# Gated cross-attention and quantized FFN on one core: softmax two steps ahead of its transposes, projections one to a step, the stage behind the attention and the first layer's order written in the source

## Chip, cores and metric

The kernel runs on one core of one Trainium2 chip. The metric is the device time of one execution in microseconds (us), start to end. The kernel before took 717.9 us, the median of three runs (715.8, 717.9, 718.52).

## What is computed

The inputs are x of 2 x 2048 rows with 512 columns, a context of 2 x 77 rows with 512 columns, two gates, and the weights. In short:

```python
x = x + tanh(g_xattn) * attention(layernorm(x), ctx, ctx, Wq, bq, Wk, bk, Wv, bv, Wo, bo)
x = x + tanh(g_ffn) * ffn(layernorm(x), w1, b1, w2, b2)
```

The attention has 16 heads of 32 columns, 77 keys, scores divided by sqrt(32), an ordinary softmax over the keys, and an output projection. The FFN has 2048 hidden columns and quantizes what it multiplies:

```python
def quant(x):
    scale = maximum(max(abs(x)), 1e-6) / 127
    return round(x / scale), scale
def qlinear(x, w, b):
    xq, sx = quant(x)
    wq, sw = quant(w)
    return (xq @ wq.T + b[None, :]) * (sw * sx)
o = qlinear(gelu(qlinear(x, w1, b1)), w2, b2)
```

The scale belongs to the whole tensor. So the first layer can start only when the maximum of all 4096 normalized rows is known, and the second only when the maximum of the whole hidden tensor is known.

## The kernel before

**Tiling.** The 4096 rows are cut into 8 blocks of 512 rows; a block is four tiles of 128 rows. The kernel has three stages: the attention over all blocks, the first layer over all blocks, the second layer over all blocks. The hidden tensor does not fit on the chip beside the rest: the last 8 of its 32 pieces are held, the other 24 go to memory (h, L611) and come back as Gb (L630).

**A block of the attention** has eight steps s (loop at L428 and L429). Step s stands for group g = s // 2 of four heads and for one half (two tiles) of the rows. What a step works on:

- softmax (L258): the scores ps on PE (L267), their maximum mx on DVE (L276), the subtraction into e on DVE (L280), the exponential on ACT (L286), the sum sm on DVE (L288), its reciprocal (L290), and the product e times rs on POOL (L291).
- transpose_a (L297), twice a step: four transposes pta of e on PE (L304), copied to aT by ACT (L305).
- project_q (L245), once for a group: four matmuls pq (L248) and a copy with bias to qT on ACT (L256).
- apply_v (L307), once for a group: pc on PE (L313), copied to cT by ACT (L321).
- project_o (L323), once for a row tile of the block before: four matmuls po (L326); DVE adds the result to x (L333).

For the next block, norm(i+1) (L222) takes the statistics of its rows on DVE (st_a and L141), and transpose_x (L229) normalizes a row tile on DVE (xn, L234), transposes it on PE (ptx, L239) and copies it to xnT on ACT (L240). At step 7, norm2_stats and norm2_max (L337, L342) take the second layernorm's statistics (st_f) of the block before and the maxima of its normalized rows: a burst of DVE work. Through weight_step (L388) DVE also prepares the FFN's weights in the odd steps of four blocks: maxima of w1 in block 1 (L374), quantization of w1 in block 2, maxima of w2 in block 3, quantization of w2 in block 4. At step 0 of blocks 2 and 4, scale_of (L148) makes the scale of the weights: a maximum over columns on DVE, a diagonal on DVE, a matmul with ones on PE that brings the 128 maxima into every row, then maximum, scale and inverse on DVE. add_bias (L242) is POOL's.

**Which step has what.** In step s the softmax of step s + 1 is issued first, then the first transposes of step s. project_q of groups 1, 2, 3 stands at steps 0, 2, 4, and that of the next block's group 0 at step 6; apply_v of the block before's group 3 at step 0 and of groups 0, 1, 2 at steps 2, 4, 6; project_o at steps 1, 3, 5, 6; norm(i+1) at step 3; transpose_x, two tiles each, at steps 5 and 6.

**What sets the order.** Each engine runs its queue in order, and the order is fixed when the program is built. For the opening, the source's order is kept on DVE and PE (manual_schedule, L409). All else is ordered by a list scheduler of the framework, which works with estimated durations; `with tc.issue_after(x)` keeps the instructions in it behind x on their engine. Tiles come from rotating pools, and a new tile waits until the last use of the one whose place it takes. In the attention PSUM has two slots for transposes (ps_t), two for projections (ps_p) and two for scores (ps_s). The pools in SBUF hold 3 of e, 5 of qT, 3 of aT, 7 of cT, 1 of xnT. The 8 places of a 1 MB block (xpool) are shared by the blocks of x and the raw weights.

**Behind the attention** (L491 to L501) come apply_v of the last group, the four project_o of block 7 and, tile by tile, their statistics and maxima. Then the rows of block 0 are made ready for the first layer: normalize_x (L526) on POOL (xs, L529), scale_of for x, and quantize_x (L539), which for block 0 goes tile by tile: multiply and add a large constant, then subtract it again so that the value is rounded (DVE L167 and L168; ACT L546 and DVE L547 for tiles 2 and 3), four transposes px on PE (L553), copy to xqT on ACT (L556).

**The first layer** (L570): for each block, 16 chunks of the hidden columns, in four groups a of four chunks. A chunk is four matmuls ph (L583), the gelu on ACT (L590), and for two chunks together the maximum hmax on DVE (L600). For the block that follows, DVE normalizes (xs, L529), quantizes in two instructions of 2048 elements (L167, L168), and copies the transposed tiles (xqT, L558); PE does the 16 transposes px (L553) wherever the scheduler puts them. px has two slots (ps_x), ph two of two banks.

**The second layer** quantizes h (ACT L636, DVE hq L637), multiplies (pf, L645), adds b2 on POOL (L659) and the product to x (DVE), and stores. It begins with the two held blocks.

Of the kernel before, what the change touches and what calls it, by code (L numbers as in the profile page):

```python
# [8 lines left out]
F32 = mybir.dt.float32  # L9
# [33 lines left out]
def tile_flamingo_gated_block(  # L43
# [50 lines left out]
    bv_sb = awts.tile([NK, D], F32, name="bv_sb")  # L94
# [5 lines left out]
    b2_sb = const.tile([P, D], F32, name="b2_sb")  # L100
# [17 lines left out]
    nc.sync.dma_start(b2_sb, b2.to_broadcast([P, D]))  # L118
# [10 lines left out]
    w1q = const.tile([P, KC, FF], BF16, name="w1q")  # L129
    w2q = const.tile([P, FC, D], BF16, name="w2q")  # L130
# [33 lines left out]

    def quantize(dst, src, inv):

        nc.vector.tensor_scalar(src, src, inv, MAGIC, ALU.mult, ALU.add)  # L167
        return nc.vector.tensor_scalar(dst, src, MAGIC, None, ALU.subtract).ins  # L168
# [5 lines left out]
    with actx:  # L174
        work = actx.enter_context(tc.tile_pool(name="work", bufs=2))
# [4 lines left out]
        kblk, vblk = [], []  # L180
        for b in range(B):
            kb = awts.tile([P, NG, RK], F32, name=f"kb{b}")
            nc.gpsimd.memset(kb, 0.0)
            kblk.append(kb)
            vblk.append(awts.tile([NK, D], F32, name=f"vb{b}"))
# [56 lines left out]
        def add_bias(i, t):  # L242
            nc.gpsimd.tensor_tensor(X[i][:, t, :], X[i][:, t, :], bo_sb, ALU.add)
# [98 lines left out]
        def norm2_max(i, t0=0, t1=NT):  # L342

            tm = small.tile([P, NT], F32, tag="tm", name=f"tm{i}_{t0}")
            for t in range(t0, t1):
                xn = work.tile([P, D], F32, tag="xn", name=f"xf{i}_{t}")
                nc.vector.tensor_scalar(
                    xn,
                    X[i][:, t, :],
                    mean2[:, i, t, 0:1],  # L350
                    rstd2[:, i, t : t + 1],
                    ALU.subtract,
                    ALU.mult,
                )
                nc.vector.tensor_reduce(
                    tm[:, t - t0 : t - t0 + 1], xn, AX.X, ALU.max, apply_absolute_value=True
                )
            k = i if t1 - t0 == NT else NB - 1 + t0
            nc.vector.tensor_reduce(xmax[:, k : k + 1], tm[:, : t1 - t0], AX.X, ALU.max)
# [67 lines left out]
        softmax(0, 0)  # L427
        for i in range(NB):  # L428
            for s in range(2 * NG):  # L429
                last = None  # L430
                if s + 1 < 2 * NG:
                    last = softmax(i, s + 1)
                    last_product = last["POOL"]
                elif i + 1 < NB:
                    last = softmax(i + 1, 0)
# [4 lines left out]
                if s == 0:  # L440
                    if i > 0:
                        apply_v(i - 1, NG - 1)
                    project_q(i, 1)
# [9 lines left out]
                if s in (2, 4):  # L453
                    project_q(i, 1 + s // 2)
                    apply_v(i, s // 2 - 1)
                if s in (1, 3, 5, 6) and i > 0:
                    project_o(i - 1, (1, 3, 5, 6).index(s))
                if s == 6:
                    apply_v(i, 2)
                if i + 1 < NB:  # L460
                    if s == 3:
                        with tc.issue_after(last["DVE"]):
                            norm(i + 1)
                    if s in (5, 6):
                        for t in (2 * s - 10, 2 * s - 9):
                            transpose_x(i + 1, t)
                transpose_a(i, s, 1)
                if s == 6 and i + 1 < NB:
                    project_q(i + 1, 0)
# [8 lines left out]
                if last is not None:  # L478
                    with tc.issue_after(last["DVE"]):
                        weight_step(i, s)  # L480
                    t = s - NT if i == 0 else s // 2
                    if t >= 0 and (i == 0 or s % 2 == 0):
                        with tc.issue_after(last["POOL"]):
                            add_bias(i, t)
# [10 lines left out]
        for t in range(NT):  # L495
            project_o(NB - 1, t)
            last = norm2_stats(NB - 1, t, t + 1)
            if t > 0:
                with tc.issue_after(last):
                    norm2_max(NB - 1, t - 1, t)  # L500
        norm2_max(NB - 1, NT - 1, NT)  # L501
# [6 lines left out]
    )  # L508

# [7 lines left out]
    with ExitStack() as fctx:  # L517
# [8 lines left out]
        def normalize_x(i, engine):  # L526
            xs = fwork.tile([P, NT, D], F32, tag="xs", name=f"xs{i}")
            for t in range(NT):
                engine.tensor_scalar(  # L529
                    xs[:, t, :],  # L530
                    X[i][:, t, :],
                    mean2[:, i, t, 0:1],
                    rstd2[:, i, t : t + 1],
                    ALU.subtract,
                    ALU.mult,
                )
            return xs

        def quantize_x(i, xs, n):  # L539

            xq = fwork.tile([P, NT, D], BF16, tag="xq", name=f"xq{i}")
            xqT = fwork.tile([P, KC, TB], BF16, tag="xqT", name=f"xqT{i}")
            for t0 in range(0, NT, n):
                v, vq = xs[:, t0 : t0 + n, :], xq[:, t0 : t0 + n, :]
                if n == 1 and t0 >= NT // 2:
                    nc.scalar.activation(v, v, AF.Copy, bias=MAGIC, scale=inv_x)  # L546
                    last = nc.vector.tensor_scalar(vq, v, MAGIC, None, ALU.subtract).ins  # L547
                else:
                    last = quantize(vq, v, inv_x)
                for t in range(t0, t0 + n):  # L550
                    px = ps_x.tile([P, KC, P], BF16, tag="px", name=f"px{i}_{t}")
                    for kc in range(KC):
                        nc.tensor.transpose(px[:, kc, :], xq[:, t, kc * P : (kc + 1) * P], identb)  # L553
                    dst = xqT[:, :, t * P : (t + 1) * P]
                    if n == 1:
                        nc.scalar.copy(dst, px)  # L556
                    else:
                        nc.vector.tensor_copy(dst, px)  # L558
            return xqT, last


        with tc.issue_after(last_product), tc.high_priority(offset=300):
            xs = normalize_x(0, nc.gpsimd)
        s_x, inv_x = scale_of(xmax, "x", ps_g, "pg")
        xqT, last = quantize_x(0, xs, 1)
# [3 lines left out]
        nc.vector.tensor_scalar(b1s, b1_sb, s1, None, ALU.mult)  # L569
        for i in range(NB):  # L570
            cur = xqT
            if i + 1 < NB:
                with tc.issue_after(last):
                    xs = normalize_x(i + 1, nc.vector)
                xqT, last = quantize_x(i + 1, xs, NT)
            for a in range(GT):
                G = gtile(f"G{i}_{a}")
                for v in range(GF // 2):
# [149 lines left out]
```

## Time and profile before

The profile is of one execution, which itself took 718.17 us; 716.2 us of it is the span from the first to the last instruction recorded. The mean TensorE clock was 0.986 of full speed.

| engine | busy us | share of the span | instructions |
|---|---|---|---|
| PE (matmul) | 662.0 | 92% | 3160 |
| PEld (weight load) | 326.6 | 46% | 3160 |
| DVE | 526.9 | 74% | 821 |
| ACT | 345.7 | 48% | 474 |
| POOL | 210.7 | 29% | 164 |

| group of instructions | count | mean ns of one |
|---|---|---|
| PE ph, first layer (L583) | 512 | 381 |
| PE pf, second layer (L645) | 512 | 386 |
| PE pq (L248) | 256 | 613 |
| PE po (L326) | 256 | 597 |
| DVE mx (L276) | 64 | 786 |
| DVE sm (L288) | 64 | 789 |
| DVE hmax (L600) | 65 | 1196 |
| ACT exp (L286) | 64 | 716 |
| ACT gelu (L590) | 128 | 777 |
| POOL product e (L291) | 64 | 1218 |
| DVE xs, first layer (L529) | 24 | 540 |
| DVE quantize, multiply and add (L167) | 7 | 1281 |
| DVE quantize, subtract (L168) | 7 | 1218 |
| DVE xqT copy (L558) | 28 | 416 |

A duration in such a row is from an instruction's start to its end, and ends of matmuls are modelled; neighbours on an engine overlap a little, so where one follows another without a pause the distance from start to start is shorter than the mean. The attention takes 0 to 429 us, its last projections 429.11 to 443.11, the first layer 457.57 to 585.07, the second the rest. By DMA 85.44 MB are moved, 119 GB/s in the mean; the 24 stores of h and their 24 loads are 1 MB each.

### The profile page before, as it was taken

To read this page: it belongs to the slowest core of one execution; us is meant where nothing else is said; L and a number is where in the kernel's file an instruction comes from. 1 tells how busy PE (TensorE), PEld (TensorE's weight loads), DVE (VectorE), ACT (ScalarE), POOL (GpSimd) and SP (SyncE) were. 2 spreads that over 40 slices of the span, in tenths; PEclk is the share of its full clock that TensorE was granted. 3 is DMA by queue.
4 is the path that set the end of the run, shared out by engine and by line. 5 is a ranking of instruction groups with operands and counts; after the bars stand their busy time and mean duration, and the time that the engine had idled before them with its cause. 6 is when DMAs were issued, how large, how long until landed. Compare 5 with 4: busy or idle time off the path is not lost.

```text
span 716.2 us, 8398 instructions
## 1 busy us (share of the span) xinstructions
PE 662.0 (92%) x3160; PEld 326.6 (46%) x3160; DVE 526.9 (74%) x821; ACT 345.7 (48%) x474; POOL 210.7 (29%) x164
## 2 busy tenths in 40 slices
PE   4998999899999999999999997699999978999977
PEld 2655445445445445454555543344444433444433
DVE  3564678889888799587577668799997669855542
ACT  2455344334344334444444440477777779454540
POOL 2134323234232342432333232300000009991000
PEclk9999999999999999999999999699999999999999
DMA  9900200121311311100000000066666107699871
GB/s 300 343 1 11 107 0 1 37 82 59 118 59 59 119 59 59 59 1 0 1 1 0 1 1 0 22 271 259 271 265 264 59 0 293 249 346 335 329 253 74
DMA packets 26432, 85.44 MB, mean 119 GB/s; under 512 B 3531, under 2 KB 3531, under 8 KB 20248
## 3 DMA queue, kind: packets, MB, share of 16 engines
q1 hardware_dynamic: 24520, 83.54, 31.0%
q10 hardware_dynamic: 1872, 1.37, 0.6%
q8 instruction: 25, 0.41, 0.2%
q14 instruction: 15, 0.12, 0.0%
HBM read 51.34 MB, written 33.55 MB: 119 GB/s over the span
## 4 chain that ended last, share of the span: by engine, by line
PE 58%; DVE 21%; DMA 7%; POOL 6%; ACT 4%; issue 3%; SPq 1%; POOLq 0%; DVEq 0%; ACTq 0%
PE ph L583 17%; PE pq L248 9%; PE po L326 8%; PE pf L645 7%; PE pta L304 6%; DMA Gb<-h 6%; PE ps L267 4%; POOL e L291 3%; DVE mx L276 3%; PE pc L313 3%; DVE sm L288 2%; DVE e L280 2%; DVE st_a L141 2%; ACT Gb L636 1%; DVE st_f L141 1%
## 5 line engine op out<-in xcount | busy, mean ns | idle before, releaser
L291 POOL TENSOR_TENSOR e<-e,rs 128x616 f32<-128x616 f32 x64 | 77.9, 1218 | 261.7 <-DVE rs L290 190.2
L583 PE MATMUL ph<-xqT,w1q 128*128 128x512 bf16 x512 | 124.2, 381 | 0.9 <-ACT xqT L556 0.7
L645 PE MATMUL pf<-w2q,hq 128*128 128x512 bf16 x512 | 114.4, 386 | 9.4 <-DVE hq L637 4.9
L248 PE MATMUL pq<-xnT,wq_sb 128*128 128x512 f32 x256 | 121.0, 613 | 0.9 <-ACT xnT L240 0.9
L305 ACT COPY aT<-pta 77x512 f32<-77x512 f32 x128 | 73.5, 580 | 93.7 <-PE pta L304 93.6
L326 PE MATMUL po<-wo_sb,cT 128*128 128x512 f32 x256 | 117.5, 597 | 0.0
L590 ACT ACTIVATE G<-ph,b1s,s 128x512 f32<-128x512 f32 x128 | 99.5, 777 | 28.9 <-PE ph L583 23.8
L659 POOL TENSOR_TENSOR x<-x,b_sb 128x512 f32<-128x512 f32 x32 | 57.9, 1853 | 135.6 <-DVE b_sb L616 135.6
L304 PE MATMUL pta<-ident,e 128*77 128x128 f32 x512 | 81.2, 284 | 13.8 <-POOL e L291 11.0
L304 PEld LDWEIGHTS pta<-ident,e 128*77 128x77 f32 x512 | 57.7, 147 | 68.1 <-POOL e L291 33.7
L600 DVE TENSOR_REDUCE hmax<-G 128x1 f32<-128x1024 f32 (+1 forms) x65 | 75.2, 1196 | 16.4 <-ACT G L590 16.1
L645 PEld LDWEIGHTS <-hq 128*128 128x128 bf16 x512 | 50.4, 99 | 73.2 <-issue 8.3
L583 PEld LDWEIGHTS <-w1q 128*128 128x128 bf16 x512 | 49.2, 97 | 67.6 <-issue 18.2
L276 DVE TENSOR_REDUCE mx<-ps 128x8 f32<-128x616 f32 x64 | 50.2, 786 | 39.9 <-PE ps L267 39.6
L248 PEld LDWEIGHTS pq<-xnT,wq_sb 128*128 128x128 f32 x256 | 46.7, 194 | 53.2 <-issue 50.2
L636 ACT ACTIVATE Gb<-Gb,inv_h 128x2048 f32<-128x2048 f32 x24 | 47.6, 1999 | 46.3 <-DMA Gb<-h 46.3
L288 DVE TENSOR_REDUCE sm<-e 128x8 f32<-128x616 f32 x64 | 50.4, 789 | 25.0 <-ACT e L286 24.4
L286 ACT ACTIVATE e<-e 128x616 f32<-128x616 f32 x64 | 45.8, 716 | 42.6 <-DVE e L280 42.5
L326 PEld LDWEIGHTS po<-wo_sb,cT 128*128 128x128 f32 x256 | 45.6, 190 | 45.0 <-issue 44.5
L637 DVE TENSOR_SCALAR hq<-Gb 128x2048 bf16<-128x2048 f32 x24 | 36.9, 1547 | 32.2 <-ACT Gb L636 32.2
L267 PE MATMUL ps<-kb,qT 64*128 64x154 f32 x512 | 55.5, 319 | 0.9 <-ACT qT L256 0.8
L256 ACT ACTIVATE qT<-pq,bq_sb 128x512 f32<-128x512 f32 x32 | 22.0, 687 | 65.5 <-PE pq L248 65.5
(90 smaller groups left out, 646.5 us busy)
## 6 DMA issues: line engine op xcount, KB each, us to landing
h<-G SPq DMA_DIRECT2D x24, 1024.0 KB, 3.8
Gb<-h SPq DMA_DIRECT2D x24, 1024.0 KB, 7.2
raw_w<-in_w2T SPq DMA_DIRECT2D x8, 1024.0 KB, 5.0
out_y<-x SPq DMA_DIRECT2D x32, 256.0 KB, 3.8
x<-in_x SPq DMA_DIRECT2D x7, 1024.0 KB, 5.0
raw_w<-in_w1T SPq DMA_DIRECT2D x4, 1024.0 KB, 9.8
x<-in_x SPq DMA_DIRECT2D x4, 256.0 KB, 6.2
wq_sb<-in_wqT ACTq DMA_DIRECT2D x1, 1024.0 KB, 10.6
```

The costliest lines, as they stand in the source:

```text
L248: nc.tensor.matmul(pq, wq_sb[:, kc, g * P : (g + 1) * P], xnT[i][:, kc, :], start=(kc == 0), stop=(kc == KC - 1),)
L267: nc.tensor.matmul(ps[:, q, u * RK : (u + 1) * RK], qT[i, g][r, t * P : (t + 1) * P], kblk[i // NBB][r, g, :], start=True, stop=True,)
L276: nc.vector.tensor_reduce(mx, sc, AX.X, ALU.max)
L288: nc.vector.tensor_reduce(sm, e4, AX.X, ALU.add)
L291: last["POOL"] = nc.gpsimd.tensor_tensor(e4, e4, rs[:, :, :, None].to_broadcast([P, 2, HG, NK]), ALU.mult).ins
L304: nc.tensor.transpose(pt[:NK, j, :], es[i, s][:, u, j, :], ident)
L305: nc.scalar.copy(aT[i, g][:, :, t * P : (t + 1) * P], pt[:NK, :, :])
L326: nc.tensor.matmul(po, cT[i, g][:, t * P : (t + 1) * P], wo_sb[:, g, :], start=(g == 0), stop=(g == NG - 1),)
L583: nc.tensor.matmul(ph[:, u, :], w1q[:, kc, fc * P : (fc + 1) * P], cur[:, kc, :], start=(kc == 0), stop=(kc == KC - 1),)
L590: nc.scalar.activation(G[:, 2 * v + u, :], ph[:, u, :], AF.Gelu, bias=b1s[:, fc : fc + 1], scale=s1,)
L600: nc.vector.tensor_reduce(hmax[:, k + u : k + u + 1], G[:, 2 * v + u : 2 * v + u + n, :], AX.XY, ALU.max, apply_absolute_value=True,)
L645: nc.tensor.matmul(po[t], hq[:, fc, t * P : (t + 1) * P], w2q[:, fc, :], start=(fc == 0), stop=(fc == FC - 1),)
```

## The change

**Attention.** Softmax of step s + 2, not s + 1, is issued first in step s; the opening has softmax(0,1) and project_q(0,1) added. apply_v and project_o go to the even steps (one each), project_q to the odd ones: groups 2 and 3 of the block at steps 1 and 3, groups 0 and 1 of the next block at steps 5 and 7. norm(i+1) moves from step 3 to step 1, and transpose_x from steps 5 and 6 to 3 and 5.

**Behind the attention.** Block 0's normalized rows xs0 are now made by DVE at step 5 of block 7, in an aT buffer. The scale of x, the quantization, the transposes (px0, in ps_t's slots) and the copies to xqT0 (in turn by ACT and DVE) are put inside the attention's pools, and issue_after ties the order of the maxima and of the first quantizations.

**First layer.** PE keeps the source's order (manual_schedule). All 16 transposes of the next block stand ahead of the block's last quarter (a == GT - 1). DVE still normalizes, quantizes and copies for the next block.

**Buffers.** b2 is loaded after the attention into memory that the attention had. The biases of v lie in a cT buffer. xqT0 is a tile of its own. kblk and vblk are only allocated earlier.

The diff, with unchanged lines mostly left out:

```diff
@@ -91,13 +91,15 @@
     ctx_sb = awts.tile([P, B, KC, NK], F32, name="ctx_sb")
-    bv_sb = awts.tile([NK, D], F32, name="bv_sb")
+    kblk = [awts.tile([P, NG, RK], F32, name=f"kb{b}") for b in range(B)]
+    vblk = [awts.tile([NK, D], F32, name=f"vb{b}") for b in range(B)]
+    work = actx.enter_context(tc.tile_pool(name="work", bufs=2))
+    bv_sb = work.tile([NK, D], F32, tag="cT", name="bv_sb", bufs=7)
     bq_sb = const.tile([P, KC], F32, name="bq_sb")
...
     b1_sb = const.tile([P, FC], F32, name="b1_sb")
-    b2_sb = const.tile([P, D], F32, name="b2_sb")
@@ -115,7 +117,6 @@
     nc.sync.dma_start(b1_sb, b1)
-    nc.sync.dma_start(b2_sb, b2.to_broadcast([P, D]))
@@ -127,6 +128,7 @@
     w1q = const.tile([P, KC, FF], BF16, name="w1q")
+    xqT0 = const.tile([P, KC, TB], BF16, name="xqT0")
     w2q = const.tile([P, FC, D], BF16, name="w2q")
@@ -162,6 +164,21 @@
+    def normalize2(dst, i, t):
+        nc.vector.tensor_scalar(
+            dst,
+            X[i][:, t, :],
+            mean2[:, i, t, 0:1],
+            rstd2[:, i, t : t + 1],
+            ALU.subtract,
+            ALU.mult,
+        )
+    def transpose_q(dst, src):
+        for kc in range(KC):
+            nc.tensor.transpose(dst[:, kc, :], src[:, kc * P : (kc + 1) * P], identb)
     def quantize(dst, src, inv):
@@ -172,17 +189,12 @@
     with actx:
-        work = actx.enter_context(tc.tile_pool(name="work", bufs=2))
         ps_s = actx.enter_context(tc.tile_pool(name="ps_s", bufs=2, space=PSUM))
...
-        kblk, vblk = [], []
-        for b in range(B):
-            kb = awts.tile([P, NG, RK], F32, name=f"kb{b}")
+        for kb in kblk:
             nc.gpsimd.memset(kb, 0.0)
-            kblk.append(kb)
-            vblk.append(awts.tile([NK, D], F32, name=f"vb{b}"))
@@ -344,19 +356,14 @@
                 xn = work.tile([P, D], F32, tag="xn", name=f"xf{i}_{t}")
-                nc.vector.tensor_scalar(
-                    xn,
-                    X[i][:, t, :],
-                    mean2[:, i, t, 0:1],
-                    rstd2[:, i, t : t + 1],
-                    ALU.subtract,
-                    ALU.mult,
-                )
+                normalize2(xn, i, t)
                 nc.vector.tensor_reduce(
...
             k = i if t1 - t0 == NT else NB - 1 + t0
-            nc.vector.tensor_reduce(xmax[:, k : k + 1], tm[:, : t1 - t0], AX.X, ALU.max)
+            return nc.vector.tensor_reduce(
+                xmax[:, k : k + 1], tm[:, : t1 - t0], AX.X, ALU.max
+            ).ins
@@ -425,22 +432,18 @@
         softmax(0, 0)
+        softmax(0, 1)
+        project_q(0, 1)
         for i in range(NB):
             for s in range(2 * NG):
-                last = None
-                if s + 1 < 2 * NG:
-                    last = softmax(i, s + 1)
-                    last_product = last["POOL"]
+                if s + 2 < 2 * NG:
+                    last = softmax(i, s + 2)
                 elif i + 1 < NB:
-                    last = softmax(i + 1, 0)
+                    last = softmax(i + 1, s + 2 - 2 * NG)
                 transpose_a(i, s, 0)
...
                     project_k(0, s + 2)
-                if s == 0:
-                    if i > 0:
-                        apply_v(i - 1, NG - 1)
-                    project_q(i, 1)
                 if i == 0 and s == 1:
@@ -450,23 +453,25 @@
                         nc.gpsimd.tensor_scalar(bo_sb, bo_sb, tg[:, 0:1], None, ALU.mult)
-                if s in (2, 4):
-                    project_q(i, 1 + s // 2)
-                    apply_v(i, s // 2 - 1)
-                if s in (1, 3, 5, 6) and i > 0:
-                    project_o(i - 1, (1, 3, 5, 6).index(s))
-                if s == 6:
-                    apply_v(i, 2)
+                if s % 2 == 0:
+                    if s > 0:
+                        apply_v(i, s // 2 - 1)
+                    elif i > 0:
+                        apply_v(i - 1, NG - 1)
+                    if i > 0:
+                        project_o(i - 1, s // 2)
+                if s in (1, 3):
+                    project_q(i, (s + 3) // 2)
                 if i + 1 < NB:
-                    if s == 3:
+                    if s == 1:
                         with tc.issue_after(last["DVE"]):
                             norm(i + 1)
-                    if s in (5, 6):
-                        for t in (2 * s - 10, 2 * s - 9):
+                    if s in (3, 5):
+                        for t in (s - 3, s - 2):
                             transpose_x(i + 1, t)
                 transpose_a(i, s, 1)
-                if s == 6 and i + 1 < NB:
-                    project_q(i + 1, 0)
+                if s in (5, 7) and i + 1 < NB:
+                    project_q(i + 1, (s - 5) // 2)
                 if i == 0 and 3 <= s < 7:
@@ -475,13 +480,17 @@
                     norm2_max(i - 1)
-                if last is not None:
-                    with tc.issue_after(last["DVE"]):
-                        weight_step(i, s)
-                    t = s - NT if i == 0 else s // 2
-                    if t >= 0 and (i == 0 or s % 2 == 0):
-                        with tc.issue_after(last["POOL"]):
-                            add_bias(i, t)
+                with tc.issue_after(last["DVE"]):
+                    weight_step(i, s)
+                    if i == NB - 1 and s == 5:
+                        xs0 = work.tile([P, NT, D], F32, tag="aT", name="xs0", bufs=3)
+                        for t in range(NT):
+                            normalize2(xs0[:, t, :], 0, t)
+                t = s - NT if i == 0 else s // 2
+                if t >= 0 and (i == 0 or s % 2 == 0):
+                    with tc.issue_after(last["POOL"]):
+                        add_bias(i, t)
             if i + 2 < NB:
@@ -497,8 +506,24 @@
                 with tc.issue_after(last):
-                    norm2_max(NB - 1, t - 1, t)
-        norm2_max(NB - 1, NT - 1, NT)
+                    last = norm2_max(NB - 1, t - 1, t)
+        with tc.issue_after(last):
+            norm2_max(NB - 1, NT - 1, NT)
+        s_x, inv_x = scale_of(xmax, "x", ps_p, "pp")
+        xq0 = work.tile([P, NT, D], BF16, tag="xnT", name="xq0", bufs=1)
+        for t in range(NT):
+            v, vq = xs0[:, t, :], xq0[:, t, :]
+            if t < NT // 2:
+                with tc.issue_after(last):
+                    last = quantize(vq, v, inv_x)
+            else:
+                nc.scalar.activation(v, v, AF.Copy, bias=MAGIC, scale=inv_x)
+                last = nc.vector.tensor_scalar(vq, v, MAGIC, None, ALU.subtract).ins
+        for t in range(NT):
+            px = ps_t.tile([P, KC, P], BF16, tag="pt", name=f"px0_{t}")
+            transpose_q(px, xq0[:, t, :])
+            copy = nc.vector.tensor_copy if t % 2 else nc.scalar.copy
+            copy(xqT0[:, :, t * P : (t + 1) * P], px)
     s_w1, s_w2 = s_w["w1"], s_w["w2"]
@@ -506,6 +531,10 @@
     )
+    late = ctx.enter_context(tc.tile_pool(name="late", bufs=1, reuse_waits="tile"))
+    b2_sb = late.tile([P, D], F32, name="b2_sb")
+    nc.sync.dma_start(b2_sb, b2.to_broadcast([P, D]))
@@ -523,58 +552,36 @@
-        def normalize_x(i, engine):
+        def quantize_x(i):
             xs = fwork.tile([P, NT, D], F32, tag="xs", name=f"xs{i}")
-            for t in range(NT):
-                engine.tensor_scalar(
-                    xs[:, t, :],
-                    X[i][:, t, :],
-                    mean2[:, i, t, 0:1],
-                    rstd2[:, i, t : t + 1],
-                    ALU.subtract,
-                    ALU.mult,
-                )
-            return xs
-        def quantize_x(i, xs, n):
             xq = fwork.tile([P, NT, D], BF16, tag="xq", name=f"xq{i}")
             xqT = fwork.tile([P, KC, TB], BF16, tag="xqT", name=f"xqT{i}")
-            for t0 in range(0, NT, n):
-                v, vq = xs[:, t0 : t0 + n, :], xq[:, t0 : t0 + n, :]
-                if n == 1 and t0 >= NT // 2:
-                    nc.scalar.activation(v, v, AF.Copy, bias=MAGIC, scale=inv_x)
-                    last = nc.vector.tensor_scalar(vq, v, MAGIC, None, ALU.subtract).ins
-                else:
-                    last = quantize(vq, v, inv_x)
-                for t in range(t0, t0 + n):
-                    px = ps_x.tile([P, KC, P], BF16, tag="px", name=f"px{i}_{t}")
-                    for kc in range(KC):
-                        nc.tensor.transpose(px[:, kc, :], xq[:, t, kc * P : (kc + 1) * P], identb)
-                    dst = xqT[:, :, t * P : (t + 1) * P]
-                    if n == 1:
-                        nc.scalar.copy(dst, px)
-                    else:
-                        nc.vector.tensor_copy(dst, px)
-            return xqT, last
-        with tc.issue_after(last_product), tc.high_priority(offset=300):
-            xs = normalize_x(0, nc.gpsimd)
-        s_x, inv_x = scale_of(xmax, "x", ps_g, "pg")
-        xqT, last = quantize_x(0, xs, 1)
+            for t in range(NT):
+                normalize2(xs[:, t, :], i, t)
+            quantize(xq, xs, inv_x)
+            return xq, xqT
+        def transpose_xq(i, xq, xqT):
+            for t in range(NT):
+                px = ps_x.tile([P, KC, P], BF16, tag="px", name=f"px{i}_{t}")
+                transpose_q(px, xq[:, t, :])
+                nc.vector.tensor_copy(xqT[:, :, t * P : (t + 1) * P], px)
         s1 = const.tile([P, 1], F32, name="s1")
...
         nc.vector.tensor_scalar(b1s, b1_sb, s1, None, ALU.mult)
+        fctx.enter_context(tc.manual_schedule(engines={mybir.EngineType.PE}))
         for i in range(NB):
-            cur = xqT
+            cur = xqT if i else xqT0
             if i + 1 < NB:
                 with tc.issue_after(last):
-                    xs = normalize_x(i + 1, nc.vector)
-                xqT, last = quantize_x(i + 1, xs, NT)
+                    xq, xqT = quantize_x(i + 1)
             for a in range(GT):
                 G = gtile(f"G{i}_{a}")
+                if a == GT - 1 and i + 1 < NB:
+                    transpose_xq(i + 1, xq, xqT)
                 for v in range(GF // 2):
...
```

## Prediction

> **What bounds the kernel now.** I read the busy times by stage first (us; then busy time and count of PE, weight loads, DVE, ACT, POOL; TensorE clock; DMA share; GB/s).
>
> ```profile
> 104.00:157.00 53.00, 50.55 (x250) 25.78 (x247) 45.41 (x79) 21.67 (x37) 18.08 (x15) 1.00 0.06 21
> ...
> 313.00:363.00 50.00, 49.12 (x241) 25.72 (x240) 35.35 (x69) 21.78 (x36) 16.66 (x14) 1.00 0.00 1
> ...
> 410.00:458.00 48.00, 35.44 (x143) 16.84 (x142) 34.47 (x74) 13.48 (x23) 18.65 (x14) 0.88 0.00 1
> 458.00:585.00 127.00, 126.75 (x624) 55.76 (x622) 109.39 (x129) 98.66 (x127) 0.00 (x0) 0.99 0.49 199
> ```
>
> PE is busy nearly throughout: attention (to 429 us) and first layer (458 to 585) are its stages. DVE is second, at 45 of 53 us in a block that also prepares weights. The second layer (585 to 716) waits for Gb loads; the change leaves its instructions and DMA order as they are.
>
> Next the chain that ended last, for the length of a block: the fourth step of blocks 1 to 6 starts norm(i+1) at
>
> ```profile
> 96.29 1.19 DVE st_a L141 x2
> ...
> 148.85 1.19 DVE st_a L141 x2
> ...
> 201.08 1.19 DVE st_a L141 x2
> ...
> 253.30 1.19 DVE st_a L141 x2
> ...
> 305.47 1.19 DVE st_a L141 x2
> ...
> 355.41 1.19 DVE st_a L141 x2
> ```
>
> Four periods of 52.2 to 52.6 us (209.2 in all), then one of 49.94 without weight work. The short one has 50 - 49.12 = 0.88 us of PE idle, so a block is 49.06 us of PE work. A long one loses 3.1 us; the waits of 157 to 209 name the largest loss:
>
> ```profile
> PE pta L304 <- POOL e L291: 2.2, 3, 1.1
> ```
>
> These are transposes that wait for the softmax of their own step. Third, the timeline behind the last projection (443.1 us) and into the first layer:
>
> ```profile
> 445.89 8.66 POOL L529 TENSOR_SCALAR xs<-x,mean,rstd 128x512 f32<-128x512 f32 x4
> ...
> 450.23 0.16 DVE L162 RECIPROCAL inv_x<-s_x 128x1 f32<-128x1 f32 x1
> ...
> 454.58 0.72 ACT L546 ACTIVATE xs<-xs,inv_x 128x512 f32<-128x512 f32 x1 [1.75 <-POOL xs L529]
> ...
> 455.81 1.91 DVE L529 TENSOR_SCALAR xs<-x,mean,rstd 128x512 f32<-128x512 f32 x4
> ...
> 457.57 4.40 PE L583 MATMUL ph<-xqT,w1q 128*128 128x512 bf16 x13 [0.67 <-ACT xqT L556]
> 457.76 1.29 DVE L167 TENSOR_SCALAR xs<-xs,inv_x 128x2048 f32<-128x2048 f32 x1
> 459.08 1.23 DVE L168 TENSOR_SCALAR xq<-xs 128x2048 bf16<-128x2048 f32 x1
> ```
>
> The scale is known at 450.4, but POOL's normalization ends only at 454.5, so L583 starts 14.5 us after the projection. DVE work is serial: 455.81, 457.76, 459.08 are back to back.
>
> **What the Trainium skill says.** "TensorE: Matmul & The Clock Gate", Part 1: after an idle window of about 3.4 us PE runs at half clock, for about as long. The trace agrees: a 3.86 us gap before 698.80 is followed by
>
> ```profile
> 698.80:702.00 3.20, 3.20 (x9) 0.55 0.22 82
> ```
>
> and a 2.6 us gap at 606 leaves the clock at 1.00. Same page, "Architectural detail": ACT and DVE are strict FIFOs; PE's queue moves only weight loads ahead. So a copy queued behind late work is late too; both layers' stalls below rest on it. "VectorE: DVE Perf Modes", "The DRAIN you can't avoid": a DVE operation does not start until the one before has left the pipe. The trace's start-to-start distances agree to a few hundredths, and I price DVE by them: mx 0.80, subtraction 0.71, sm 0.70, 512-element normalization 0.48, quantize 1.22 and 1.15, hmax 1.15, weight maximum 2.2.
>
> **The change, part by part**, by the instruction order of the built program.
>
> *Softmax two steps ahead.* Each transpose now has a full further step (some 6 us) for its e, so the POOL waits go. What is late next? From block 2's timeline: a bias copy qT lets its scores start 0.94 us after the projection (176.81 to 177.75); a transpose slot (two of them) is free 0.83 us after the transposes (171.95 to 172.78). In the new order scores follow a projection with only 0.77 us of PE work between at two steps: 2 x 0.17. At s=5 pta, ptx, ptx, pta, pq use the two slots without a break: 0.33 + 0.09 + 0.23; at s=3 another 0.18. Together 1.16 us a block, so 49.06 + 1.16 = 50.2.
>
> DVE is the second danger. norm(i+1) moves from s=3 to s=1, just behind the norm2 burst of s=7. Placing block 3 by hand from the start of step 7 of block 2: the burst ends at 9.8, the subtractions of steps 2 to 5 of block 3 end at 12.4, 15.6, 24.2 and 29.0. ACT has the exp of softmax 5 ahead of the copy qT of group 3, so that copy starts at 29.8, not 28.4: 1.35 us of PE wait. In blocks 2 and 4 the scale's matmul stands in PE's order right behind a transpose, but its diagonal comes from DVE 1.2 us later. So 1.2 + 1.35 + 1.2 = 3.75 for blocks 2 to 4; bounds 0 (DVE as early as the scheduler thought) and 9 (three steps as late as when I use whole durations, 3 us each). Block 5 has the burst but no weights: none. norm(5) needs the load of x5, freed by the last weight maximum; landing takes 5.0 us (DMA table), DVE arrives after about 6: nothing, 1 us at worst.
>
> Sum: four long periods 4 x 50.2 + 3.75 = 204.6 against 209.2, -4.6. Two short ones +0.3 each. From 36 to 96 us the PE timeline shows 3.1 us of named waits; 1.6 of the new kind remain, -1.5. Block 7: consecutive transposes without work between, +0.4. **Attention -5.1.** The projections are moved, not multiplied.
>
> *The stage behind.* xs0 (4 x 0.48 on DVE) runs in block 7, where DVE is busy 32 of 47 us: free; without that cover 1.9. The maxima of rows 2 and 3 no longer alternate, inverse scale 0.4 us earlier, 6.9 us after the projection. Then on DVE in its order: s1, xs0 row 0, b1s, xq row 0, xs0 row 1, row 2, xq row 1, row 3: to 10.65. Transpose 3 needs the slot of row 1, whose copy is behind these: 11.05; its own copy ends at 11.85, L583 starts at 11.9 against 14.46. **-2.6** (bounds -1.5, -3.6).
>
> *First layer's order.* Before, PE put the 16 transposes of block i+1 between matmuls and DVE copied them unnoticed (a block is 15.85 us: 64 x 0.236 = 15.13, and 0.72 of transposes). Now all stand before the last quarter, and the third and fourth wait for the copies of the first and second: two slots, DVE alone copies. Let zero be the start of L583, when DVE is free too. PE reaches the transposes at 48 x 0.236 + 1.4 (cold clock, as before) = 12.8. But ahead of the first copy DVE has, in order: xs1 (1.95), 8 normalizations of 512 (3.85), five quantize halves (6.0), five hmax (5.75): 17.55, and the copy ends at 17.95. Another hmax and the second copy: 19.5; PE goes on at 19.75 instead of 13.65. **+6.1**; that gap is over 3.4 us, so the clock falls: +1.4. In the other six blocks DVE has caught up: px0 is complete 0.4 us after the transposes start, copy 0.4, px2, the same for px3: 1.5 instead of 0.85, 6 x 0.65 = 3.9. **+11.4.** Bounds: 8 (start 2 us later on a colder clock, no second fall) to 14. Nothing recovers it: PE sets the end of this stage.
>
> *b2's load* moves to after attention: it is the last on SP's queue before the first store of h, waits for PE's last use of that memory (before 443), and is needed at 589: nothing. The biases of v in a cT buffer: seven suffice, nothing.
>
> Sum: -5.1 - 2.6 + 11.4 = +3.7. Profiled span 716.2 + 3.7, and 1.97 around it (718.17 in all) gives 721.9; that run is 0.27 above the median, so **721.6**. That is 0.5% slower, about the least that a measurement here tells from no change.
>
> **Rivals.** (1) Not slower: attention runs at PE's floor. DVE is never late at ACT and slots free sooner: long periods 49.5 (-11.2), short -0.4 each, opening -2: -14, total -5.2, **712.7**. It decides once attention gains over 8.8 us, that is, when long blocks fall under 50.0. For it: 3.1 us a block are idle and a step is a long lead. Against: DVE's 45 us must fit in 50, and ACT is a FIFO. (2) DVE becomes the bound: from s=7 to s=3 some 33 us of DVE work meet 30 us of PE; with 3 us of stall in each of blocks 2 to 4, and as much in the rest of the long periods as before, attention gains nothing: **728**. (3) The first layer does not stall at first: DVE's loads fall behind the copies in time because L583 starts late enough; then only 4.6, **714.8**. Against: the order is fixed at build, and durations of equal shapes are measured.
>
> **How the numbers follow.** Forecast 0.50 (own range 718 to 726, a little over half of it over +0.5%), rival 1 0.15, rival 2 0.22, rival 3 0.08, others 0.05. Faster by over 0.5% (under 714.3): most of rival 1, part of 3: 0.16. Slower by over 0.5% (over 721.5): 0.27 + 0.22 + 0.02 = 0.51. Between: 0.33. The range 713 to 729 takes in rivals 2 and 3 and the upper part of 1.
>
> **What would show it.** Attention: POOL e vanishes from PE's waits; instead ACT qT, ACT aT and xnT; periods 50 to 51.5. Behind it: no POOL xs, L583 11 to 13 us after the projection. First layer: px waiting for DVE, one gap of 5 to 6 us in its first block with the clock at 0.5 after, some 0.65 in the others, stage 11 us longer. Wrong if the first-block gap is under 3 us, or if long periods are under 49.8 or over 52.

## The result, and the profile after

The changed kernel takes 774.5 us, the median of four runs (772.37, 773.22, 775.86 and one of 1771.12), against 716.85 us of the kernel before in the same session. The run of 1771 us, whose cause is not known, is left out of the ratio, which is 1.080 (interval 1.0744 to 1.0851). The prediction was 721.6 us with a range of 713 to 729, so it was wrong, by 53 us. The profiled execution took 775.86 us, of it 773.7 us span: 57.5 us more than the span before.

Four marks split the span: the start of the last four project_o, the first and the last matmul of the first layer, the end.

| stretch | before, us | after, us | difference | forecast |
|---|---|---|---|---|
| attention, to the last projections | 0 to 429.1 | 0 to 424.8 | -4.3 | -5.1 |
| end of the projections to first layer | 14.5 | 11.1 | -3.4 | -2.6 |
| first layer | 127.5 | 192.3 | +64.8 | +11.4 |
| second layer | 131.1 | 131.5 | +0.4 | 0 |

First, who waited for whom in the whole profile of the changed kernel (us in total, times, longest):

```profile
PE ph L590 <- ACT G L597: 55.6, 64, 0.9
...
PE px L180 <- DVE xqT L569: 3.4, 8, 1.2
```

The first line is the result: PE waits 64 times, once for every tile of two chunks, 0.87 us each, for the gelu. The second is what the prediction had put in its place, PE waiting for DVE's copies: 3.4 us.

The timeline of the changed kernel in the first layer (start, length, engine, group, idle time before it and who ended it):

```profile
501.73 1.89 PE L590 MATMUL ph<-xqT,w1q 128*128 128x512 bf16 x8 [0.87 <-ACT G L597]
...
502.79 1.64 ACT L597 ACTIVATE G<-ph,b1s,s 128x512 f32<-128x512 f32 x2 [1.11 <-PE ph L590]
...
504.48 1.89 PE L590 MATMUL ph<-xqT,w1q 128*128 128x512 bf16 x8 [0.87 <-ACT G L597]
...
505.54 1.64 ACT L597 ACTIVATE G<-ph,b1s,s 128x512 f32<-128x512 f32 x2 [1.11 <-PE ph L590]
```

PE does eight matmuls (the second chunk of one tile and the first of the next) and stops. It goes on at 504.48, when the gelu of the last of these chunks, the second of ACT's two, has ended (502.79 + 1.64 = 504.43). Why it stops is in the built program: the first matmul of a tile's second chunk waits for ACT's count after the gelu of that tile's first chunk. Both chunks belong to one tile, ph, and in this program a write to a tile that another engine has read waits for the reader, though the halves do not overlap. The program before has the same wait, for each of its 64 tiles. But there the scheduler had put PE's chunks in the order A0, B0, A1, B1 of two tiles A and B, so four matmuls of B lay over the gelu of A0. The source's order is A0, A1, B0, B1: nothing lies over it. The same stretch before shows 28 matmuls in a row without a named wait, and a pair of gelus every 1.89 us in place of 2.75:

```profile
499.75 6.70 PE L583 MATMUL ph<-xqT,w1q 128*128 128x512 bf16 x28
...
501.84 1.64 ACT L590 ACTIVATE G<-ph,b1s,s 128x512 f32<-128x512 f32 x2 [0.25 <-PE ph L583]
...
503.73 1.64 ACT L590 ACTIVATE G<-ph,b1s,s 128x512 f32<-128x512 f32 x2 [0.25 <-PE ph L583]
```

The attention. The chain of waits of the changed kernel, at the fourth project_o of each block, and PE's waits from 36 to 420 us:

```profile
116.83 3.65 PE po L338 x8
...
168.98 3.63 PE po L338 x8
...
220.03 3.65 PE po L338 x8
...
272.18 3.63 PE po L338 x8
...
323.23 3.63 PE po L338 x8
...
374.27 3.63 PE po L338 x8
```

```profile
PE ptx L251 <- ACT aT L317: 2.0, 7, 0.6
PE pq L260 <- ACT xnT L252: 1.3, 7, 0.2
PE pta L316 <- ACT aT L317: 1.0, 3, 0.3
PE pg_w L158 <- DVE diag_w L156: 0.4, 2, 0.2
```

POOL e is gone from the waits; 4.7 us are left, against 13.5 us before in the same stretch, most of it this:

```profile
PE pta L304 <- POOL e L291: 11.0, 18, 1.5
```

Yet the periods are 52.15, 51.05, 52.15, 51.05 and 51.04 us, and the last is longer than the short one before (49.94). So PE works longer for the same instructions: the busy times of the fifth and sixth stretch (columns as in the prediction) say 50.6 us where a block was 49.1 us.

```profile
272.18:323.23 51.05, 50.62 (x242) 26.15 (x241) 38.12 (x70) 21.19 (x36) 16.66 (x14) 1.00 0.08 28
323.23:374.27 51.04, 50.61 (x241) 26.14 (x241) 36.40 (x68) 21.40 (x36) 16.66 (x14) 1.00 0.00 1
```

The group that has grown is pc (apply_v), and PE's timeline shows how:

```profile
371.51 1.04 PE L325 MATMUL pc<-aT,vb 77*32 77x512 f32 x2
372.49 0.80 PE L279 MATMUL ps<-kb,qT 64*128 64x154 f32 x8
373.21 1.06 PE L325 MATMUL pc<-aT,vb 77*32 77x512 f32 x6
```

The scheduler cut the four products with v into one and three, with scores between. One takes 0.98 us to the next start and three take 0.99 (each product has two records), and in the kernel before all four together took 1.00:

```profile
313.06 1.07 PE L313 MATMUL pc<-aT,vb 77*32 77x512 f32 x8
314.06 0.66 PE L304 MATMUL pta<-ident,e 128*77 128x128 f32 x4
```

The four use different 32-column parts of the array and run side by side, so a cut costs a full product. In the trace 13 of 32 groups are cut, two of each block from 1 to 6 and one of block 0; before, none. The Trainium skill, "TensorE: Matmul & The Clock Gate", Part 3 ("Packing small matmuls"), describes products in different column parts running at once; this trace agrees, with 1.00 us for four and 0.98 for one.

### The profile page after: what moved, and what is told of

Same layout as the page of the kernel before. It is cut to its first block, busy times and chain, and to the rows that moved or that the text cites. A ratio compares the mean times of both kernels' runs of the same rounds, so it can differ in the third digit from the quotient of the medians.

```text
span 773.7 us, 8392 instructions
## 1 busy us (share of the span) xinstructions
PE 674.8 (87%) x3160; PEld 331.4 (43%) x3160; DVE 532.1 (69%) x827; ACT 342.8 (44%) x472; POOL 200.6 (26%) x160
## 4 chain that ended last, share of the span: by engine, by line
PE 69%; ACT 10%; DVE 9%; DMA 8%; issue 2%; SPq 1%; POOL 0%; ACTq 0%; DVEq 0%
PE ph L590 16%; PE po L338 14%; PE pq L260 14%; PE pta L316 7%; DMA Gb<-h 7%; ACT G L597 7%; PE ps L279 5%; PE pc L325 5%; PE pf L652 4%; ACT Gb L643 2%; PE ptx L251 2%; DVE hq L644 1%; DMA x<-in_x 1%; DVE x L670 1%; PE px L180 1%
## 5 line engine op out<-in xcount | busy, mean ns | idle before, releaser
L590 PE MATMUL ph<-xqT,w1q 128*128 128x512 bf16 x512 | 126.3, 388 | 56.1 <-ACT G L597 55.6
L607 DVE TENSOR_REDUCE hmax<-G 128x1 f32<-128x1024 f32 (+1 forms) x65 | 78.0, 1202 | 71.5 <-ACT G L597 71.4
L260 PE MATMUL pq<-xnT,wq_sb 128*128 128x512 f32 x256 | 119.0, 609 | 2.0 <-ACT xnT L252 2.0
L316 PE MATMUL pta<-ident,e 128*77 128x128 f32 x512 | 79.4, 280 | 1.7 <-ACT aT L317 1.2
L316 PEld LDWEIGHTS pta<-ident,e 128*77 128x77 f32 x512 | 59.8, 147 | 40.6 <-issue 34.3
L288 DVE TENSOR_REDUCE mx<-ps 128x8 f32<-128x616 f32 x64 | 49.9, 780 | 30.3 <-PE ps L279 30.1
L644 DVE TENSOR_SCALAR hq<-Gb 128x2048 bf16<-128x2048 f32 x24 | 38.5, 1615 | 31.3 <-ACT Gb L643 31.3
L279 PE MATMUL ps<-kb,qT 64*128 64x154 f32 x512 | 52.7, 319 | 0.2
L292 DVE TENSOR_TENSOR e<-ps,mx 128x616 f32<-128x616 f32 x64 | 50.9, 796 | 2.9
```

The lines of the kernel that those rows point to most:

```text
L260: nc.tensor.matmul(pq, wq_sb[:, kc, g * P : (g + 1) * P], xnT[i][:, kc, :], start=(kc == 0), stop=(kc == KC - 1),)
L279: nc.tensor.matmul(ps[:, q, u * RK : (u + 1) * RK], qT[i, g][r, t * P : (t + 1) * P], kblk[i // NBB][r, g, :], start=True, stop=True,)
L316: nc.tensor.transpose(pt[:NK, j, :], es[i, s][:, u, j, :], ident)
L590: nc.tensor.matmul(ph[:, u, :], w1q[:, kc, fc * P : (fc + 1) * P], cur[:, kc, :], start=(kc == 0), stop=(kc == KC - 1),)
L607: nc.vector.tensor_reduce(hmax[:, k + u : k + u + 1], G[:, 2 * v + u : 2 * v + u + n, :], AX.XY, ALU.max, apply_absolute_value=True,)
```

## Experiments

"Span" is the profiled execution's. Each ratio is to the kernel before, timed on the same chip.

**splitph**: the wait taken away, the order kept.

```diff
-ph = ps_h.tile([P, 2, TB], F32, tag="ph", name=f"ph{i}_{a}_{v}")
 for u in range(2):
+    ph = ps_h.tile([P, TB], F32, tag="ph", name=f"ph{i}_{a}_{v}_{u}")
```

(with bufs=4 in place of 2: the same memory.)

> The changed kernel with one tile per chunk of the first layer (four of one bank in place of two of two banks); the matmuls' order stays that of the source. Theory A (in the source's order a chunk's matmuls follow the other chunk of the same tile and wait for its gelu, 64 times 0.87 us): the 55.6 us of PE waiting for ACT G are gone, the span falls from 773.7 to about 718, some us more if DVE's copies then come late (as the prediction had it), so 716 to 726. Theory B (the copies of the transposed tiles by DVE, or ACT's and PE's use of the same memory in this order, cost the time): the order of the matmuls and the copies are the same as before, so the first layer stays near 192 us and the time above 760.

Measured: 712.07 us, ratio 0.992 (0.9887 to 0.9950), span 709.5. PE ph no longer waits for ACT G at all; the first layer takes 130.4 us. Same order, same number of banks, no wait: what cost the time was that both chunks were one tile, not the memory. Theory B falls. The span is 6.5 us under the expected range, since the waits cost more than the idle time says: a tile took 2.75 us in the changed kernel, and eight matmuls take 1.73 us here, a difference of 65 us in 64 tiles and not 55.6.

```profile
464.15 13.98 PE L590 MATMUL ph<-xqT,w1q 128*128 128x512 bf16 x64
...
479.86 0.39 PE L180 MATMUL px<-identb,xq 128*128 128x128 bf16 x4 [1.29 <-DVE xqT L569]
481.32 0.38 PE L180 MATMUL px<-identb,xq 128*128 128x128 bf16 x4 [1.07 <-DVE xqT L569]
```

The first line is a whole block: (13.98 - 0.38) / 63 = 0.216 us from matmul to matmul, not 0.236. Behind it the waits for DVE's copies are there now, 9.6 us in all.

**nomanual**: the scheduler's order again, two-chunk tiles kept.

```diff
-fctx.enter_context(tc.manual_schedule(engines={mybir.EngineType.PE}))
```

> The changed kernel without the source's order on PE in the first layer; the tiles of two chunks stay. Theory A: the scheduler puts a chunk of the other tile between the two chunks of a tile, the gelu is hidden again, the first layer takes 127 to 131 us and the whole is 773.7 - 62 = 712, so 709 to 716, faster than the kernel before by what attention (4.2) and the stage behind it (3.4) gained. Theory B: the copies are still DVE's alone and from two slots; the first layer keeps at least 11 us of loss, 720 or more.

Measured: 711.63 us, ratio 0.991 (0.9869 to 0.9946), span 707.4, first layer 129.9 us. As theory A has it.

**before_order**: one line added to the kernel before.

```diff
+fctx.enter_context(tc.manual_schedule(engines={mybir.EngineType.PE}))
 for i in range(NB):
     cur = xqT
```

> The kernel before with the source's order on PE in the first layer, nothing else. Theory A: 64 waits of 0.87 us, first layer 127 + 56 = 183 us or a little more, the whole 773 to 780. Theory B (the transposes at the last quarter, the moved normalization or the buffers): this kernel has none of them, so it stays within 10 us of 718.

Measured: 781.15 us, ratio 1.088 (1.0838 to 1.0922). The wait is the same to a tenth:

```profile
PE ph L584 <- ACT G L591: 55.5, 64, 0.9
PE pta L304 <- POOL e L291: 11.0, 18, 1.5
```

POOL e, the attention's wait, is what it was. The time is 1 us over the expected range: the first layer takes 189.4 us, and it also begins 4 us later (461.8), since in the source of that kernel the transposes of block 1 stand ahead of block 0's matmuls. One line, without any other part of the change, makes 61.9 of the first layer's 64.8 us.

**keeppc**: splitph, and the second to fourth product with v under a higher priority.

```diff
-nc.tensor.matmul(pc[r, :], ...)
+with tc.high_priority(offset=60 if j else 0):
+    nc.tensor.matmul(pc[r, :], ...)
```

> As splitph, and the four products of a group with v are kept together on PE by a higher priority for the second to fourth. In the changed kernel 13 of 32 groups are cut into one and three by the scores, and the trace shows 1.0 us for each part where the whole takes 1.0 to 1.1 us. Theory: 13 times 1.0 us less than splitph, 13 us, periods of the attention 49.0 to 49.6 in place of 51.05. Rival (PE is the bound by its count of matmuls, and the periods of 51.05 come from waits for slots and copies): less than 3 us.

Measured: 706.19 us, ratio 0.983 (0.9795 to 0.9862), span 702.1, no group cut. A gain of 7.4 us of span over splitph, little more than half of the 13. The period without weight work fell as expected, by 1.95 us to 49.10; those with weight work did not all:

```profile
165.66:215.65 49.99, 48.98 (x241) 25.90 (x241) 43.07 (x72) 20.95 (x36) 16.77 (x14) 1.00 0.28 93
215.65:268.61 52.96, 50.93 (x243) 26.74 (x243) 45.32 (x79) 21.19 (x36) 17.66 (x14) 0.97 0.20 73
...
318.17:367.27 49.10, 48.66 (x241) 25.91 (x241) 36.59 (x67) 21.33 (x36) 16.64 (x14) 1.00 0.00 1
```

In the period of 52.96 us, DVE's burst of norm2 and a maximum of w2 (2.27 us) come one after the other; the next softmax's subtraction is late, ACT's exponential behind it, and the copy aT behind that: PE pta waits 1.38 us for ACT aT at 233.82. That is the late DVE that the prediction described. The changed kernel's period at that place was 1.1 us over its base of 51.05; this one is 3.9 us over 49.10. That the cut products had been the cover fits this, but was not tested by itself.

The wait is not all of the 3.9 us. The same stop stands two blocks earlier, at 132.57 (that period is 51.27 us), and the projection pq behind it took 3.60 us there and 5.29 here:

```profile
132.57 0.34 PE L316 MATMUL pta<-ident,e 128*77 128x128 f32 x1 [1.38 <-ACT aT L317]
...
133.45 3.60 PE L260 MATMUL pq<-xnT,wq_sb 128*128 128x512 f32 x8
...
233.82 0.33 PE L316 MATMUL pta<-ident,e 128*77 128x128 f32 x1 [1.38 <-ACT aT L317]
...
234.70 5.29 PE L260 MATMUL pq<-xnT,wq_sb 128*128 128x512 f32 x8
```

```profile
134.00:136.00 2.00, 2.00 (x6) 1.00 0.00 0
...
235.00:237.00 2.00, 2.00 (x3) 0.50 0.16 59
```

Behind the second stop the granted clock was 0.50, behind the first 1.00: 1.7 us of the 3.9 are slower matmuls.

**before_splitph**: splitph's edit on the kernel before.

> The kernel before with one tile per chunk in the first layer, nothing else. Theory: the kernel before already has the wait for the gelu of its own tile: eight matmuls of the other tile's and its own chunk take 1.887 us there and 8 x 0.2153 = 1.722 us where nothing stops them, so 0.165 us per tile, 64 times, 10.5 us. Without it the first layer is at PE's 14.5 us a block, or at DVE's 14.9 (eight hmax of 1.15, normalization 1.85, quantization 2.35, four copies 1.5): 127.5 falls to 118 to 122 us, the whole to 709 to 713. Rival: 0.236 us is the pace of PE with this shape, as the prediction took it, and the shorter step of splitph has to do with its order: 716 to 719.

Measured: 711.62 us, ratio 0.993 (0.9913 to 0.9955), first layer 121.0 us against 127.5. So the kernel before had the wait too; 0.236 was not PE's pace.

**spread**: keeppc, with the weights' steps moved away from step 7.

```diff
-j, odd = divmod(s, 2)
+j = {1: 0, 3: 1, 4: 2, 5: 3}.get(s, 0)
+odd = s in (1, 3, 4, 5)
```

> As keeppc (tiles split, the four products with v kept together), and the DVE work on the weights moved from steps 1, 3, 5, 7 to steps 1, 3, 4, 5, away from the burst of step 7. Theory: keeppc lost 5.6 us of its 13 to a late DVE: in its blocks 2 to 5 the periods are 51.27, 49.99, 52.96 and 49.56 where block 6 has 49.10, and PE waits for ACT's copies behind a late exponential. Then blocks 2 and 4 fall to about 50.2 (1.1 us of the scale's matmul stay), the whole by 2 to 5 us against keeppc. Rival: the rest is the scale and the waits for slots, which this doesn't touch: within 1 us of keeppc.

Measured: 700.52 us, ratio 0.978 (0.9759 to 0.9800), span 699.6. The periods from 113.02 us on are 49.90, 49.10, 49.90, 49.10, 49.10; the first layer starts 7.1 us earlier than in keeppc and 14.1 earlier than in splitph. In span the gain is 2.5 us. Weight work on top of the burst was the cause; the two periods that are 0.8 us longer are those with the scale's matmul. The second layer gave 4 us back (133.2 us against 129.3 in keeppc). No edit touches it, and in the other runs it takes 128 to 133 us; why is open.

```profile
212.02:261.92 49.90, 49.22 (x244) 26.23 (x243) 45.29 (x80) 21.48 (x36) 17.64 (x14) 1.00 0.21 70
...
311.02:360.12 49.10, 48.66 (x241) 25.90 (x241) 36.59 (x67) 21.34 (x36) 16.64 (x14) 1.00 0.00 1
```

**lead1**: spread, with the softmax one step ahead.

```diff
-softmax(0, 1)
 project_q(0, 1)
...
-if s + 2 < 2 * NG:
-    last = softmax(i, s + 2)
+if s + 1 < 2 * NG:
+    last = softmax(i, s + 1)
 elif i + 1 < NB:
-    last = softmax(i + 1, s + 2 - 2 * NG)
+    last = softmax(i + 1, 0)
```

> As spread, but the softmax is issued one step ahead of its transposes, as in the kernel before; the projections stay one to a step. Theory: the two steps are what took PE's 11.0 us of waiting for POOL's e away; with one step they come back, 8 to 13 us more than spread, POOL e named as what PE waits for. Rival: the even spread of the projections gives POOL its time already: under 3 us more, and no POOL e in the waits.

Measured: 720.92 us, ratio 1.004 (1.0019 to 1.0054), span 719.3: 19.7 us more than spread, more than expected. PE waits for the softmax again:

```profile
PE pta L316 <- POOL e L303: 16.2, 22, 2.5
```

The five periods that I compared are 1.8 to 2.7 us longer. The stretch from the last of their marks to the first layer is 8.4 us longer: 5.2 us of it are waits for POOL e, and the last projections behind them ran slower (15.82 us against 14.00; the granted clock was 0.50 from 432 to 434 us, behind a stop of 2.47 us). With the projections spread as they are, the lead of two steps is what makes the attention faster; their spread alone does not.

**poolxs**: keeppc, with POOL in place of DVE for the normalized rows of blocks 2 to 7 and three slots for px (normalize2 gets an engine as argument).

```diff
-normalize2(xs[:, t, :], i, t)
+normalize2(xs[:, t, :], i, t, nc.gpsimd if i > 1 else nc.vector)
```

> As keeppc, and in the first layer POOL makes the normalized rows of blocks 2 to 7 in place of DVE, and the transposes have three slots. Theory: once the gelu's wait is gone DVE is the bound there, 14.9 us of work a block against 14.5 on PE, and PE waits 9.6 us for its copies; with 13.0 us of DVE work the first layer falls from 130.8 to 117 to 122 us, so 9 to 13 us less than keeppc. Rival: the copies are late because of their place in DVE's order or because POOL slows DVE: less than 3 us, or a loss.

Measured: 718.86 us, ratio 1.003 (1.0016 to 1.0051), a loss against keeppc. DVE's order has the quantization of a later block ahead of hmax and copies that are due, and now it waits for POOL (2.15 us a tile):

```profile
479.21 1.29 DVE L184 TENSOR_SCALAR xs<-xs,inv_x 128x2048 f32<-128x2048 f32 x1 [6.19 <-POOL xs L169]
```

```profile
485.39 0.59 PE L180 MATMUL px<-identb,xq 128*128 128x128 bf16 x4 [13.15 <-DVE xqT L570]
```

Less work on DVE is of no use where its order makes it wait; whether POOL would do with another order was not tried.

**best1**: spread and poolxs together.

> spread and poolxs together. If both act where their theories say, in stages that do not touch, the gains add: keeppc less 11 to 18 us, 688 to 695.

Measured: 713.55 us, ratio 0.994 (0.9917 to 0.9958): the loss of poolxs is larger than the gain of spread.

**copies**: spread, and in transpose_xq

```diff
-nc.vector.tensor_copy(xqT[:, :, t * P : (t + 1) * P], px)
+copy = nc.vector.tensor_copy if t % 2 else nc.scalar.copy
+copy(xqT[:, :, t * P : (t + 1) * P], px)
```

with three slots for px.

> As spread, and in the first layer the copies of the transposed tiles go in turn to ACT and DVE, with three slots in place of two. Theory: of the 9.6 us that PE waits for DVE's copies there most is left over from one engine's queue (hmax of 1.15 us ahead of a copy), so the first layer falls from 131 by 5 to 9 us. Rival: ACT is as full (16 gelus of 0.8 us in 15 us) and a copy waits behind a gelu there as long as behind an hmax: within 2 us of spread.

Measured: 691.97 us, ratio 0.963 (0.9603 to 0.9665), span 691.0. PE's wait for DVE's copies falls from 9.6 us in spread to 3.7 here, and the first layer from 131.4 to 124.0 us:

```profile
PE px L180 <- DVE xqT L571: 9.6, 10, 2.6
...
PE px L180 <- DVE xqT L572: 3.7, 6, 1.4
```

What ACT's copies and what the third slot gave was not told apart. This is the best version: 3.7% faster than the kernel before.

## Why the prediction was wrong

**First layer's order: the step that failed.** The prediction took the change there for one of the transposes alone ("Before, PE put the 16 transposes of block i+1 between matmuls", "64 x 0.236 = 15.13") and never asked in which order PE had the chunks. The source's order undoes A0, B0, A1, B1, and 64 gelus come onto PE's path: 64 x 0.865 = 55.4 us (2.752 us a tile against 1.887). With longer stops at the transposes (2.8 us in the first block and 1.45 in each of six, 11.5 in all, against seven times 0.75 before) and some 3 us more at half clock at the start, that is the 64.8.

The trace before held the hint. The pace of 0.236 us was measured right and read wrong: in the single records of the trace it is eight matmuls at 0.2153 us and one stop of 0.165 us, about the wait of 1.03 us (2.752 - 8 x 0.2153) less the 0.861 us of the other tile's four matmuls. The weight loads show the eights, 1.89 us apart:

```profile
500.78 1.61 PEld L583 LDWEIGHTS <-w1q 128*128 128x128 bf16 x8 [0.28 <-issue]
...
502.67 1.61 PEld L583 LDWEIGHTS <-w1q 128*128 128x128 bf16 x8 [0.28 <-issue]
```

The Trainium skill, "TensorE: Matmul & The Clock Gate", "Back-to-back issue gap", gives two figures for this shape: 512/2.4 + 2.5 = 216 ns for a matmul by itself, and about 131 ns in a sustained stream of weight loads and matmuls. splitph, which is such a stream, shows 0.216 us; no run here shows 131 ns. A pace above both asked for a reason.

**The copies behind DVE.** The forecast was 6.1 us in the first block and 0.65 in each of six. The changed kernel shows 1.6 us (0.45 + 1.17) in its first block: as PE was slowed by the gelus, DVE had caught up. The prediction's own sign against it, a first-block gap under 3 us, came true. The other six blocks are as forecast: 1.45 us at the transposes against 0.75 before. In splitph the waits come to 9.6 us, most of them in the second to fourth block, but there DVE's order is another too. So the mechanism is there, while the large place was not the one worked out; that the sum is near the forecast 10 is luck. The order that was worked out was not run with a fast PE.

**Attention, -5.1 against -4.3: right in sum by luck, wrong in its terms.** The POOL wait went, as lead1 shows from the other side. Slots cost about 0.4 us a block, not 1.16 (51.05 - 50.62). A late DVE cost at most 2.2 us, not 3.75: the two periods with the scale's matmul are 1.1 us longer, about half of it idle time, and block 3's is not. These two periods, 52.15 us, are over the 52 that the prediction had named as a sign against it. Against these, 13 cuts of apply_v cost 1 us each, which no step named: PE's 49.06 us of work a block was taken to be fixed, and it depends on what stands between the four products. Without the cuts and with the weights' steps moved (run spread), periods are 49.1 to 49.9: rival 1, PE's floor, was within reach.

**The stage behind, -2.6 against -3.4:** right; POOL xs is gone, and the first layer starts 11.1 us after the projections (forecast 11.9). **b2 and second layer, 0:** right within 0.4 us.

**A reading of the trace.** DVE's prices held, but a normalization, recorded as 0.54 us, is followed by the next after 0.46 (four of them in 1.91 us, at 455.81). The trace agrees with the sentence on the DVE pipe to under a tenth of a microsecond, not to a few hundredths.

**Rivals.** None named this. Rival 3's time (714.8) is near what splitph and nomanual gave, but by another way.

## What to carry to other kernels

When a change fixes an engine's order by the source, write down the order that the scheduler had and ask for every neighbour that is parted what it had been covering; here it was two chunks of different tiles, and the cost was 64 times a gelu. Give each unit that another engine reads its own tile, as here a tile was waited for as a whole. And compare a measured pace with the shape's own pace before using it as a price: the difference is a wait that may grow.

## What was not expected of the hardware

Four fp32 products with 32 output columns each take 1.00 us together and 0.98 us for one alone, so what stands between them decides the cost: 1.95 us a block for two cuts (51.05 to 49.10 us). And a pause of 0.165 us in eight matmuls, too short for the waits to name, was worth 6.5 us of the first layer when it was taken away in the kernel before.

The prediction took a gap of over 3.4 us as what makes PE's clock fall. In these runs the length of a stop alone does not decide it: the two stops of 1.38 us in keeppc, alike in what surrounds them, were followed by a clock of 1.00 and of 0.50, and a stop of 2.56 us was followed by 1.00 in splitph (at 498.53) and by 0.51 in spread (at 483.68). What decides is open. A short stop can thus cost more than its length: 1.7 us more for 1.38.
